# Batches 6 and 7 wholly by seven block products, denser two-batch products, and the last results stored by quarters

## The chip, the cores and the metric

The kernel runs on one core of a Trainium2 chip. The metric is the device time of one execution in microseconds, as the median of several runs. A core has a matrix engine (TensorE, PE in the profile; its weight loads are listed as PEld), VectorE (DVE), ScalarE (ACT), GpSimd (POOL) and SyncE (SP). Matrix products are written to PSUM, a small memory from which VectorE or ScalarE copies them to SBUF; DMA moves data between SBUF and device memory. A DMA is issued by an instruction in the queue of an engine, here SyncE, ScalarE or GpSimd (SPq, ACTq, POOLq).

## The reference

There are 8 batches of 1024 rows with 512 features, float32. A small network on the conditioning vector makes, per batch, a 512 x 512 matrix; a second layer scales its inputs and outputs per batch:

```python
# layer 0, per batch b
ae = layernorm(cond, ln_g, ln_b)
h  = gelu(ae @ w1 + b1)
x_a, x_b = split(h @ w2 + b2)              # each (8, 512, rank 8)
layer = base_layer + x_a @ x_b.T           # per batch
x = x + (x + x @ layer)                    # outer and inner residual
# layer 1, per batch b
ys = cond / sqrt(512)
d  = rsqrt((ys * ys) @ (weight * weight) + 1e-8)
x  = x + ((x * ys[b]) @ weight) * d[b]
```

Both layers are linear in x once the condition is known, so out[b] = x[b] @ Q[b], with one 512 x 512 matrix Q[b] per batch: (2 I + base + rank-8 term) times N[b], where N[b] = I + diag(ys) weight diag(d).

## The kernel before, in words

A float32 product is made of three fast ones. Each operand is split into a high part (rounded by a ScalarE cast) and the rest (a VectorE subtraction), and high x high, high x rest and rest x high are added up in PSUM. Every helper that prepares an operand therefore costs a cast and a subtraction.

**Setup (to about 81 us).** The conditioning network, the low-rank factors, and the matrices Q of batches 0 to 3 are made, the last three by `Base` with plain products.

**Main loop.** A step `i` is one tile of 128 rows: `main(b, t)` runs 4 chunks x 3 = 12 matmuls of 512 columns into a PSUM tile `po`, ScalarE copies it to `o`, and ScalarE issues the store. `load_x` fetches half a batch of x (1 MB, SyncE) and `split_x` splits two tiles. Other work is hung behind steps by `at(*place(i), f, ...)`: it is emitted after `main` of step i.

**Two-batch products (`Pair`).** Batches (4, 5) and (6, 7) share the left matrix, so their two matrices N form, side by side, a product of 2 x 2 blocks that needs seven block products instead of eight (`ORDER`, 14 units of 6 matmuls of 512 columns, tiles `pp`). The list `spots` gives the step behind which each unit is emitted. Ahead of a product, `early` makes its N blocks (VectorE), `prepare` forms their difference, rounds it and subtracts. The rounded operands have two buffers (`right_tiles`, tags `nh` and `nl`), so a product's operands can be made when the product two before it is over. After the last unit, `rank_term` adds the rank-8 term of each batch, and `split_p` splits Q into `ph` and `pl`.

**Seven block products (`Seven`).** Near the end the same scheme is used on the rows: half a batch (512 rows) is a product of 2 x 2 blocks, done by seven products of 12 matmuls of 256 columns (tiles `sw`, `sz`, `sv`). `make_sums` and `make_right` prepare the right side from Q; `make_left(g)` prepares half g, in six steps; `part(g, steps)` runs the seven products in the order 1, 5, 6, 2, 7, 3, 4 and takes one step of the next half's `make_left` after each. Products 1, 6, 7 and 4 accumulate in one bank (`w`; two banks, one per 128 rows, in the last part), 5 and 3 in bank `z`, 2 in bank `v`; after each product its running sum is copied out (ScalarE `copy` for 1, 5, 6, 4; VectorE `tensor_add` for 2, 7, 3). After product 3 the half `o1` is stored, after product 4 the half `o2`, by ScalarE. The raw sums share one buffer (tag `sums`).

Before, batches 0 to 5 and the first half of batch 6 go through the main loop (52 steps), and three halves through `Seven`: batch 6's second half, and both halves of batch 7.

**Order.** A build-time scheduler orders each engine's instructions by program order and readiness. Matmuls always keep program order. For VectorE, ScalarE and SyncE, `ve`, `se` and `sy` keep it only while `InOrder.on` is true: in setup, in `early`, and again in the closing parts. `late_pools` frees the pools of the making of Q and opens those of `Seven` in their place, along with a second output pool. Tiles named `big` (x, its split halves, Q, `xa`) share nine slots; `ph` and `pl` have two each.

Of the kernel before, what the change touches and what calls it, by code (L numbers as in the profile page):

```python
# [14 lines left out]
P = 128  # L15
NB = 8
NT = 1024
D = 512
# [12 lines left out]
def cond_resid_kernel(ctx: ExitStack, tc: tile.TileContext, small, cond, condrows, consts,  # L31
# [32 lines left out]
    ve, se, sy = InOrder(nc.vector), InOrder(nc.scalar), InOrder(nc.sync)  # L64
# [14 lines left out]
    def big_tile(name, dtype=F32):  # L79
        return big.tile([P, KC, D], dtype, tag="big", name=name)  # L80
# [82 lines left out]
    def newton_rsqrt(v, sd, shape, name):  # L163

        r = sp.tile(shape, F32, name=f"r_{name}")
        ve.reciprocal(r, sd)
        t = sp.tile(shape, F32, name=f"t_{name}")
        ve.tensor_mul(t, r, r)
        ve.tensor_mul(t, t, v)
        ve.tensor_scalar(t, t, -0.5, 1.5, ALU.mult, ALU.add)  # L170
        return r, t
# [12 lines left out]
    r, t = newton_rsqrt(ve_l, sd, [NB, 1], "l")  # L184
# [102 lines left out]
    r, t = newton_rsqrt(v, sv, [P, KC, NB], "d")  # L287
# [359 lines left out]
    def p_tiles(b):  # L647
        ph[b] = ppool.tile([P, KC, D], F32R, tag="ph", name=f"ph_{b}")
        pl[b] = ppool.tile([P, KC, D], F32R, tag="pl", name=f"pl_{b}")
# [13 lines left out]
    def load_x(b, h):  # L663
        raw[b, h] = big_tile(f"x_{b}_{h}")
        sy.dma_start(raw[b, h], x[b, h])

    def split_x(b, j, part=None):

        t = raw[b, j // 2][:, :, (j % 2) * 2 * P:(j % 2 + 1) * 2 * P]
        if part != 1:  # L670
            xs[b, j] = big.tile([P, 2, KC, 2 * P], F32R, tag="big", name=f"xs_{b}_{j}")
            se.copy(xs[b, j][:, 0], t)
        if part != 0:
            ve.tensor_sub(xs[b, j][:, 1], t, xs[b, j][:, 0].bitcast(F32))
# [136 lines left out]
    def main(b, t):  # L811
        s = xs[b, t // 2]
        at = slice((t % 2) * P, (t % 2 + 1) * P)
        ps = po.tile([P, D], F32, tag="po", name=f"po_{b}_{t}")
        for c in range(KC):
            for i, (u, m) in enumerate(((0, ph[b]), (0, pl[b]), (1, ph[b]))):
                mm(ps, s[:, u, c, at], m[:, c, :],
                   start=(c == 0 and i == 0), stop=(c == KC - 1 and i == 2))
        o = pools["o"].tile([P, D], F32, tag="o", name=f"o_{b}_{t}")
        se.copy(o, ps)  # L820
        nc.scalar.dma_start(out[b, t * P:(t + 1) * P, :], o)

    class Seven:
# [28 lines left out]
            self.right = {5: (h[:, 0], t[:, 0]), 6: (h[:, 1], t[:, 1]), 7: (h[:, 2], t[:, 2]),  # L852
                          4: (h[:, 3], t[:, 3])}

        def make_right(self, whole):

            b = self.b
            for rows, cols in ((slice(0, 4), slice(0, HD)), (slice(2, 4), slice(HD, D))):
                if whole:
                    break  # L860
                se.copy(ph[b][:, rows, cols], q[b][:, rows, cols])
                ve.tensor_sub(pl[b][:, rows, cols], q[b][:, rows, cols],
                              ph[b][:, rows, cols].bitcast(F32))
            for p, rows, cols in ((1, slice(0, 2), slice(0, HD)), (2, slice(2, 4), slice(0, HD)),
                                  (3, slice(2, 4), slice(HD, D))):
                self.right[p] = ph[b][:, rows, cols], pl[b][:, rows, cols]
# [49 lines left out]
        def part(self, g, steps=(), last=False):  # L916

            b, bank, steps = self.b, {}, iter(steps)
            o1, o2 = (pools["late"].tile([P, 2, D], F32, tag="o2", name=f"o{i}_{b}_{g}", bufs=3)
                      for i in range(2))  # L920
            for p in self.ORDER:
                key = {5: "z", 3: "z", 2: "v"}.get(p, "w")
                first = p in (1, 5, 2)
                if first:
                    pool, tag = (po, "po") if key == "z" else (acc, "acc")
                    bank[key] = [pool.tile([P, 2, HD], F32, tag=tag, name=f"s{key}{i}_{b}_{g}")
                                 for i in range(2 if key == "w" and last else 1)]
                self.product(g, p, bank[key], first)
                o, cols = {1: (o1, slice(0, HD)), 2: (o1, slice(0, HD)), 3: (o1, slice(HD, D)),
                           6: (o1, slice(HD, D)), 4: (o2, slice(0, HD)), 5: (o2, slice(HD, D)),  # L930
                           7: (o2, slice(HD, D))}[p]
                for m, u in enumerate(bank[key]):
                    u, to = (u, slice(0, 2)) if len(bank[key]) == 1 else (u[:, 0:1], slice(m, m + 1))
                    if p in (2, 3, 7):
                        ve.tensor_add(o[:, to, cols], u, o[:, to, cols])
                    else:
                        se.copy(o[:, to, cols], u)
                    if p in (3, 4):
                        self.store(o, g, int(p == 4), to)
                next(steps, None)  # L940

        def store(self, o, g, half, ms):
            at = g * HT + 2 * P * half
            se.dma_start(
                out[self.b, at + P * ms.start:at + P * ms.stop, :].rearrange("(m p) d -> p m d", p=P),
                o[:, ms, :])

    def late_pools():
        making.close()
# [3 lines left out]
    NTT = NT // P  # L953
    after = {}

    def at(b, t, f, *args):
        after.setdefault((b, t), []).append((f, args))
# [5 lines left out]
    place = lambda i: divmod(i, NTT)  # L963
# [4 lines left out]
        for j in range(2):  # L968
            at(*place(first + 3 + j), split_p, b, j)

    for b, spots in ((4, [11 + n for n in range(14)]), (6, [28 + 2 * n // 3 for n in range(14)])):
        first, end = spots[0], spots[-1] + 1
        at(*place(first - 9), load_d, b)
        at(*place(first - 6), new_pair, b)
        for n, p in enumerate(Pair.ORDER):
            spot = spots[2 * n]
            at(*place(spot - 5), lambda b=b, p=p: pairs[b].early(p))
            at(*place(spot - 2), lambda b=b, p=p: pairs[b].prepare(p))
        for spot in spots:
            at(*place(spot), lambda b=b: pairs[b].unit())  # L980
        at(*place(first + 2), load_rank, b)
        at(*place(first + 4), load_rank, b + 1)
        at(*place(end), rank_term, b)
        at(*place(end + 1), rank_term, b + 1)
    for b, spot in ((4, 26), (5, 33), (6, 41)):
        for j in range(2):
            at(*place(spot + j), split_p, b, j)
    sevens = [Seven(NB - 2), Seven(NB - 1)]
# [2 lines left out]
        for _ in sevens[i].make_left(g):  # L991
            pass

    at(*place(40), late_pools)
    at(*place(42), sevens[0].make_sums)
    at(*place(43), sevens[0].make_right, True)
    at(*place(44), load_x, NB - 2, 1)
    at(*place(45), sevens[1].make_sums)
    at(*place(47), all_left, 0, 1)
    at(*place(48), sevens[1].make_right, False)  # L1000
    at(*place(48), load_x, NB - 1, 0)

    HALF = NTT // 2
    TILES = (NB - 1) * NTT - HALF
    for i in range(TILES):
        b, t = divmod(i, NTT)
        if t == 0:
            p_tiles(b + 1)
        main(b, t)
        if t % 4 == 0 and i + 4 < TILES:  # L1010
            load_x(*divmod(i // 4 + 1, NHALF))
        if t % 2 == 0 and i + 4 < TILES:
            split_x(*divmod(i // 2 + 2, NTT // 2))
        for f, args in after.get((b, t), ()):
            f(*args)
    load_x(NB - 1, 1)
    InOrder.on = True
    sevens[0].part(1, sevens[1].make_left(0))
    sevens[1].part(0, sevens[1].make_left(1))
    sevens[1].part(1, last=True)  # L1020
# [69 lines left out]
```

## Time and profile before

| | |
|---|---|
| median of 3 runs | 302.38 us (302.2 to 302.98) |
| the profiled execution | 302.37 us |
| its span, first to last instruction | 300.6 us |
| mean granted TensorE clock | 0.997 |
| TensorE busy | 293.9 us, 98% of the span |
| VectorE, ScalarE, GpSimd busy | 206.0 (69%), 152.8 (51%), 34.8 (12%) |
| chain that ended last | PE 87%, DVE 5%, DMA 4%, ACT 2% |
| one step of the main loop (12 matmuls) | 2.72 us |
| one unit of a two-batch product (6 matmuls) | 1.36 to 1.40 us |
| one of the seven products of a half (12 matmuls) | 1.44 us |
| stores of 256 KB, issue to landing, median | 2.6 us |
| stores of 512 KB | 2.9 us |

In rows of the trace, the first number is the start, the second the length (microseconds from the start of the span), then engine, line, operation, output<-input, shape. A bracket at the end is idle time of the engine just before, with what ended it. Nearly all calls on VectorE, ScalarE and SyncE pass through line 62 and matmuls through line 45, so the tile names tell them apart. ACTq and SPq rows are DMA issues. Rows by stretch of time give, for each engine, its busy share and number of instructions (PE, PEld, DVE, ACT, POOL), then the granted clock, the DMA engines' busy share and GB/s. Ends of matmuls are modelled.

### The profile page before, as it was taken

How to read it: one execution, taken by the hardware profiler on the slowest of the kernel's cores; microseconds unless marked ns; L12 is line 12 of the kernel's file. 1: busy time of each engine (PE TensorE's matmuls, PEld its weight loads, DVE VectorE, ACT ScalarE, POOL GpSimd, SP SyncE). 2: the span in 40 equal slices, each digit the busy share in tenths (PEclk: the TensorE clock that was granted, in tenths of full speed). 3: DMA queues.
4: the chain of work that ended last, by engine and by line, in shares of the span. 5: the costliest groups of instructions: out<-in, count | busy, mean ns of one | idle time of the engine just before them, and what ended most of it. 6: DMA issues, size and time to landing. Idle time of an engine off the chain costs nothing.

```text
span 300.6 us, 3913 instructions
## 1 busy us (share of the span) xinstructions
PE 293.9 (98%) x1465; PEld 226.1 (75%) x1465; DVE 206.0 (69%) x303; ACT 152.8 (51%) x224; POOL 34.8 (12%) x74
## 2 busy tenths in 40 slices
PE   8999999999999999999999999999999999999993
PEld 3655465467878778888888778888887888899993
DVE  4779840979569999873564699855628379948721
ACT  4757132246556554575654444467532655653530
POOL 0011000057104550100000081000000000000000
PEclk9999999999999999999999999999999999999998
DMA  6999999696619986534525158243351729322133
GB/s 205 406 429 416 403 424 415 218 336 180 203 70 293 309 293 195 173 99 180 174 81 202 70 157 250 83 168 104 149 209 70 226 66 358 128 101 94 48 140 140
DMA packets 18995, 62.12 MB, mean 207 GB/s; under 512 B 2704, under 2 KB 2960, under 8 KB 14624
## 3 DMA queue, kind: packets, MB, share of 16 engines
q1 hardware_dynamic: 6064, 38.78, 35.2%
q10 hardware_dynamic: 9136, 16.78, 14.8%
q0 software_dynamic: 3776, 6.31, 8.0%
q8 instruction: 11, 0.18, 0.2%
q14 instruction: 8, 0.07, 0.1%
HBM read 44.02 MB, written 17.84 MB: 206 GB/s over the span
## 4 chain that ended last, share of the span: by engine, by line
PE 87%; DVE 5%; DMA 4%; ACT 2%; issue 0%; ACTq 0%
PE po L45 48%; PE pp L45 13%; PE pq L45 7%; PE sw L45 5%; DMA w<-in_w 4%; PE px L45 3%; PE sz L45 3%; PE warm L45 2%; PE pg L45 2%; DVE n L62 2%; PE sv L45 1%; PE pr L45 1%; PE pt_t L45 1%; ACT work L62 1%; DVE scr L62 0%
## 5 line engine op out<-in xcount | busy, mean ns | idle before, releaser
L45 PE MATMUL po<-ph,xs 128*128 128x512 f32 x416 | 134.3, 392 | 0.0
L45 PEld LDWEIGHTS po<-ph,xs 128*128 128x128 f32 x416 | 78.1, 188 | 18.0 <-issue 1.7
L45 PE MATMUL po<-pl,xs 128*128 128x512 f32 x208 | 81.1, 390 | 0.0
L62 ACT COPY o<-po 128x512 f32<-128x512 f32 x52 | 30.5, 586 | 58.0 <-PE po L45 58.0
L45 PEld LDWEIGHTS po<-pl,xs 128*128 128x128 f32 x208 | 39.1, 188 | 8.0
L62 DVE TENSOR_TENSOR xs<-x,xs 128x1024 fp32r<-128x1024 f32 x26 | 31.5, 1221 | 10.5 <-ACT xs L62 10.4
L62 ACT CAST xs<-x 128x1024 fp32r<-128x1024 f32 x26 | 27.0, 1051 | 2.6 <-DMA x<-in_x 1.3
L62 DVE TENSOR_TENSOR q<-pr,q 128x512 f32<-128x512 f32 x32 | 20.1, 684 | 7.4 <-PE pr L45 7.4
L62 DVE TENSOR_TENSOR nl_p<-n,nh_p 128x1024 fp32r<-128x1024 f32 x14 | 17.1, 1223 | 10.2 <-ACT nh_p L62 10.2
L62 DVE TENSOR_TENSOR pl<-q,ph 128x1024 fp32r<-128x1024 f32 (+1 forms) x16 | 18.8, 1189 | 6.9 <-ACT ph L62 6.8
L511 POOL DMA_DIRECT2D fa<-kept_a x28 | 13.7, 508 | 72.8 <-PE pr L45 72.7
L45 PE MATMUL pq<-nh,bh 128*128 128x512 f32 x48 | 19.8, 412 | 0.0
L45 PE MATMUL pq<-nl,bh 128*128 128x512 f32 x48 | 19.1, 398 | 0.1
L45 PE MATMUL pq<-nh,bl 128*128 128x512 f32 x48 | 19.0, 395 | 0.0
L62 DVE SCALAR_TENSOR_TENSOR n<-w_sb,ysT,d 128x512 f32<-128x512 f32 x24 | 17.8, 747 | 1.0 <-DMA d<-d_out 1.0
L62 ACT COPY q<-pp 128x512 f32<-128x512 f32 x20 | 11.8, 588 | 10.9 <-PE pp L45 10.9
L62 ACT CAST ph<-q 128x1024 fp32r<-128x1024 f32 (+1 forms) x16 | 16.2, 1027 | 2.1 <-DVE q L62 2.0
L45 PE MATMUL px<-w,hT 128*32 128x512 f32 x128 | 16.0, 601 | 0.1
L62 ACT CAST nh_p<-n 128x1024 fp32r<-128x1024 f32 x14 | 14.7, 1052 | 1.6 <-PE pp L45 1.6
L45 PEld LDWEIGHTS pq<-nh,bh 128*128 128x128 f32 x48 | 9.0, 188 | 8.4 <-issue 5.0
L511 POOL DMA_DIRECT2D ft<-kept_t x28 | 13.8, 519 | 5.0 <-DMA kept_t<-st_t 5.0
L62 ACT COPY o<-sw 128x512 f32<-128x512 f32 (+1 forms) x12 | 5.7, 480 | 15.7 <-PE sw L45 10.0
(185 smaller groups left out, 465.9 us busy)
## 6 DMA issues: line engine op xcount, KB each, us to landing
w<-in_w SPq DMA_DIRECT2D x16, 1024.0 KB, 10.8
x<-in_x SPq DMA_DIRECT2D x16, 1024.0 KB, 5.3
out<-o ACTq DMA_DIRECT2D x54, 256.0 KB, 2.6
out<-o ACTq DMA_DIRECT2D x5, 512.0 KB, 2.9
ft<-kept_t POOLq DMA_DIRECT2D x28, 64.0 KB, 3.0
fa<-kept_a POOLq DMA_DIRECT2D x28, 64.0 KB, 3.3
d<-d_out POOLq DMA_DIRECT2D x6, 256.0 KB, 4.6
w_sb<-in_weight SPq DMA_DIRECT2D x2, 512.0 KB, 5.4
```

The source lines that it names most:

```text
L45: tc.keep_in_program_order(nc.tensor.matmul(*args, **kw))
L62: return lambda *a, **kw: pin(f(*a, **kw)) if InOrder.on else f(*a, **kw)
L511: nc.gpsimd.dma_start(fold[name, b][32 * c:32 * c + 32, :], kept[name, g][32 * i:32 * i + 32, :])
```

## The change

Six things are edited.

- The main loop has 48 steps: batch 6's first half goes through `Seven` too, so four parts follow the loop. `p_tiles` of batches 6 and 7 is called by `make_right`, no longer by the loop, and `make_right` has lost its argument: before, it copied nothing for batch 6, whose `ph` and `pl` came from `split_p`; now it fills the three blocks that the products need for both batches.
- The units of the first pair are emitted behind steps 11 to 20 (before: 11 to 24), those of the second behind steps 24 to 32 (before: 28 to 36). `split_p` of batch 4 moves from steps 26, 27 to 27, 28; that of batch 6 goes.
- `late_pools` and `make_sums` of batch 6 come four steps earlier, its `make_right` two, `make_sums` of batch 7 three. `make_left` of batch 6's first half is emitted behind step 43, and x of batch 6 is loaded behind steps 42 and 46.
- After the loop `InOrder.on` is set; then come the load of batch 7's first half of x, part 0 of batch 6 (with `make_left` of its second half between its products), the load of batch 7's second half, `make_right` of batch 7, and the three parts that were there before. `make_right` of batch 7 stood behind step 48 before, with the order free.
- In the last part each finished quarter of results is stored on its own: that of product 2, the two row blocks of product 7 and the quarter of product 3 by SyncE, the two row blocks of product 4 by ScalarE. Before, ScalarE stored one whole half after product 3 and two row blocks after product 4.
- `store` takes the queue and the columns as arguments.

```diff
-        def make_right(self, whole):
+        def make_right(self):
             b = self.b
+            p_tiles(b)
             for rows, cols in ((slice(0, 4), slice(0, HD)), (slice(2, 4), slice(HD, D))):
-                if whole:
-                    break
                 se.copy(ph[b][:, rows, cols], q[b][:, rows, cols])
                 ve.tensor_sub(pl[b][:, rows, cols], q[b][:, rows, cols],
                               ph[b][:, rows, cols].bitcast(F32))
...
-                    if p in (3, 4):
-                        self.store(o, g, int(p == 4), to)
+                    if last and p in (2, 3, 7, 4):
+                        self.store(se if p == 4 else sy, o, g, int(p in (4, 7)), to, cols)
+                    elif p in (3, 4):
+                        self.store(se, o, g, int(p == 4), to, slice(0, D))
                 next(steps, None)
-        def store(self, o, g, half, ms):
+        def store(self, queue, o, g, half, ms, cols):
             at = g * HT + 2 * P * half
-            se.dma_start(
-                out[self.b, at + P * ms.start:at + P * ms.stop, :].rearrange("(m p) d -> p m d", p=P),
-                o[:, ms, :])
+            queue.dma_start(
+                out[self.b, at + P * ms.start:at + P * ms.stop, cols].rearrange("(m p) d -> p m d", p=P),
+                o[:, ms, cols])
...
-    for b, spots in ((4, [11 + n for n in range(14)]), (6, [28 + 2 * n // 3 for n in range(14)])):
+    for b, spots in ((4, [11 + 3 * n // 4 for n in range(14)]), (6, [24 + 2 * n // 3 for n in range(14)])):
...
-    for b, spot in ((4, 26), (5, 33), (6, 41)):
+    for b, spot in ((4, 27), (5, 33)):
         for j in range(2):
             at(*place(spot + j), split_p, b, j)
...
-    at(*place(40), late_pools)
-    at(*place(42), sevens[0].make_sums)
-    at(*place(43), sevens[0].make_right, True)
-    at(*place(44), load_x, NB - 2, 1)
-    at(*place(45), sevens[1].make_sums)
-    at(*place(47), all_left, 0, 1)
-    at(*place(48), sevens[1].make_right, False)
-    at(*place(48), load_x, NB - 1, 0)
-    HALF = NTT // 2
-    TILES = (NB - 1) * NTT - HALF
+    at(*place(36), late_pools)
+    at(*place(38), sevens[0].make_sums)
+    at(*place(41), sevens[0].make_right)
+    at(*place(42), load_x, NB - 2, 0)
+    at(*place(42), sevens[1].make_sums)
+    at(*place(43), all_left, 0, 0)
+    at(*place(46), load_x, NB - 2, 1)
+    TILES = (NB - 2) * NTT
     for i in range(TILES):
         b, t = divmod(i, NTT)
-        if t == 0:
+        if t == 0 and i + NTT < TILES:
             p_tiles(b + 1)
...
+    InOrder.on = True
+    load_x(NB - 1, 0)
+    sevens[0].part(0, sevens[0].make_left(1))
     load_x(NB - 1, 1)
-    InOrder.on = True
+    sevens[1].make_right()
     sevens[0].part(1, sevens[1].make_left(0))
     sevens[1].part(0, sevens[1].make_left(1))
     sevens[1].part(1, last=True)
```

## The prediction

> **What bounds the kernel now.** I read the page's first rows, then the chain of waits in order of time, then ScalarE, VectorE and DMA in the last 30 us. TensorE holds the chain; from 81 us on, pieces of it follow each other without a gap:
>
> ```profile
> PE 293.9 (98%) x1465; PEld 226.1 (75%) x1465; DVE 206.0 (69%) x303; ACT 152.8 (51%) x224; POOL 34.8 (12%) x74
> ```
> ```profile
> 254.93 10.88 PE po L45 x48
> 265.81 1.43 PE sw L45 x12
> 267.25 1.44 PE sz L45 x12
> 268.69 1.44 PE sw L45 x12
> 270.12 1.44 PE sv L45 x12
> 271.57 1.44 PE sw L45 x12
> 273.00 1.44 PE sz L45 x12
> 274.44 2.88 PE sw L45 x24
> ...
> 296.63 0.37 ACT o L62
> ```
>
> The columns are start and length. `po` are tiles of batch rows (48 matmuls = 4 tiles = 10.88 us, so 2.72 a tile); from 265.81 the seven block products of a half batch run, 1.44 us each. Only two kinds of edit can move the end: fewer TensorE microseconds or new waits on TensorE, and the tail after its last matmul, which ends at 296.04 (the last starts at 295.76 and is listed with 0.28); the span ends at 300.6, so the tail is 4.56 us.
>
> **1. Four tiles become seven products: -0.8 us.** 10.88 us go; 7 x 1.44 = 10.08 come ((296.04 - 265.81) / 21 products = 1.44). Here a rule speaks for more: the Trainium skill ("TensorE: Matmul & The Clock Gate", Back-to-back issue gap) gives 518 cycles at 2.4 GHz for 512 columns and 262 for 256, so 48 x 0.216 - 84 x 0.109 = 10.36 - 9.17 = -1.19. The rows have 0.227 and 0.120, some 11 ns over the page on each matmul, and the short form pays that 84 times instead of 48. I take the rows. The granted clock is 1.00 in all of these stretches, so neither side changes speed. On the helpers this step removes two `split_x` (1.05 ScalarE, 1.22 VectorE each), `split_p` of batch 6, four 0.59 us copies and four 256 KB stores, and adds `make_left(0)` (ScalarE 1.05 + 0.62 + 2 x 1.05 = 3.8; VectorE 4 x 0.69 + 3 x 1.22 + 0.69 = 7.1), four copies, three 0.69 us adds and two 512 KB stores. That is covered by the last tiles 43 to 47, 13.6 us; see the rival on the slower side for when it isn't.
>
> **2. `make_right` of batch 7 moves into the seam between the two halves of batch 6: +1.2 us.** Before, it stood after tile 48, unpinned, and ran at 259.45 on ScalarE and 260.73 on VectorE, under `po` tiles. Now it is pinned behind part 0 and ahead of part 1. It issues casts of 1024 and 512 elements and their two subtractions, no DMA. What it is put in front of is shown by the part that begins at 265.81 (ScalarE, then VectorE; start, length):
>
> ```profile
> 267.28 0.59 ACT L62 COPY o<-sw 128x512 f32<-128x512 f32 x1 [0.85 <-PE sw L45]
> 267.76 1.05 ACT L62 CAST xa<-x 128x1024 fp32r<-128x1024 f32 x1
> 268.71 0.62 ACT L62 CAST x<-x 128x512 fp32r<-128x512 f32 x1
> 269.23 0.59 ACT L62 COPY o<-sz 128x512 f32<-128x512 f32 x1
> 269.71 1.06 ACT L62 CAST sh<-sraw 128x1024 fp32r<-128x1024 f32 x1
> 270.66 0.60 ACT L62 COPY o<-sw 128x512 f32<-128x512 f32 x1
> ```
> ```profile
> 273.35 0.68 DVE L62 TENSOR_TENSOR o<-sw,o 128x512 f32<-128x512 f32 x1
> 273.95 0.68 DVE L62 TENSOR_TENSOR x<-x,x 128x512 fp32r<-128x512 f32 x1
> 274.55 0.68 DVE L62 TENSOR_TENSOR o<-sz,o 128x512 f32<-128x512 f32 x1
> 275.15 1.22 DVE L62 TENSOR_TENSOR sl<-sraw,sh 128x1024 fp32r<-128x1024 f32 x1
> ```
>
> Products 1, 6, 7 and 4 gather in one PSUM bank, and each may start only when the result before it has been copied out. So three margins exist: product 6 starts at 268.69, and copy 1 is done at 267.87 (0.82 spare); product 7 starts at 271.57, copy 6 is done at 271.26 (0.31); product 4 starts at 274.44, VectorE's add of product 7 is done at 274.03 (0.41). ScalarE is packed from copy 1 to copy 6, so what comes ahead of copy 1 reaches copy 6 whole. Count from the start of part 0, using this part as template: ScalarE ends part 0's last store at 11.11 (276.92 - 265.81). Its two casts then take 11.15 to 12.62 (issue steps 0.95 and 0.52, as above), so copy 1 of part 1 starts at 12.62 instead of 11.54: 1.08 late. Copy 6 is 1.08 late too and has 0.31 to spare: TensorE loses 0.77. That is the low end. VectorE adds to it: its subtractions wait for the first cast (12.2) and end at 14.0, the sums S1 and S2 that the cast `sh` needs end at 15.4, so `sh` runs at 15.43, copy 6 ends at 17.0 instead of the 15.8 at which product 7 was due: 1.2 lost. VectorE is then still late: its add of product 7 ends at 20.1, where product 4, already shifted, wants it at 19.9; 0.2 more. The high end is 1.45, some 1.6 if a stopped TensorE needs 0.05 at each of three restarts. I take 1.2: the ScalarE row alone is certain, VectorE's part hangs on S1 and S2 not having been issued ahead. Part 2 absorbs the rest: its first copy, at 23.0, finds ScalarE free at 22.8.
>
> **3. The tail: -1.3 us.** Now ScalarE holds the big last store (first row) ahead of both last copies, and the DMA engines carry 1 MB at once (second fence: busy share and GB/s close each row):
>
> ```profile
> 295.41 0.38 ACTq L62 DMA_DIRECT2D out<-o  x1
> 295.83 0.37 ACT L62 COPY o<-sw 128x256 f32<-128x256 f32 x1 [5.14 <-DVE o L62]
> 296.23 0.35 ACTq L62 DMA_DIRECT2D out<-o  x1
> 296.63 0.37 ACT L62 COPY o<-sw 128x256 f32<-128x256 f32 x1 [0.42 <-ACT o L62]
> 297.03 0.35 ACTq L62 DMA_DIRECT2D out<-o  x1
> ```
> ```profile
> 296.00:297.00 1.00, 0.04 (x1) 0.00 (x0) 0.00 (x0) 0.57 (x2) 0.00 (x0) 1.00 0.69 260
> 298.50:299.00 0.50, 0.00 (x0) 0.00 (x0) 0.00 (x0) 0.00 (x0) 0.00 (x0) 0.95 1.03 389
> 299.00:299.50 0.50, 0.00 (x0) 0.00 (x0) 0.00 (x0) 0.00 (x0) 0.00 (x0) 0.50 0.12 41
> ```
>
> The last store is issued at 297.03 and lands 2.5 later (299.53); 1.07 follow to the span's end. Afterwards half of `o1`, and `o2`'s product-7 half, have gone on SyncE's queue, which has nothing else then but x loads long issued. Product 3's quarter goes there too (issue 0.38, data near 296.3 to 297.0). On ScalarE: last matmul 296.04, copy 296.16 to 296.53, issue at 296.57, 0.46 earlier. Its 128 KB meet idle engines. Lone 256 KB stores under the `po` tiles land in 2.0; their data runs 0.67 of that, so half the bytes give an estimate of 1.7. Landing 298.25 against 299.53: -1.3. The upper bound of the gain is this; for the lower, rows of 1 KB might move no faster than the 86 KB `sm` load (1.9 to landing), and one queue could delay another by 0.2: -0.9. A rule speaks against this edit: the skill ("DMA: Bandwidth & Descriptors", Issuing engines are not separate DMA queues) has all queues on the same 16 engines, so that another issuer saves issue time only. By it alone the gain would be the 0.46; the rest comes from bytes being sent earlier, which the saturated windows here show is worth something.
>
> **4. Edits I cost at nothing.** The pairs: same 14 units of 1.36 us, same rank terms (0.68 of TensorE each with the slow restart). Operands of a product can be rounded only when the product two before it is done; at 14 units in 9 tiles that leaves 8.16 us for a 1.05 cast and a 1.22 subtraction, and the second pair already runs at that density from 182.5 to 226.4 with no gap. The first goes from 14 tiles to 10, 10.9 and 8.2 us of room, while VectorE was busy 24.2 of 33 us there; one late cast would cost its 1.05. The x loads move past nothing on SyncE that waits; 16 of them go out, the last two at 246.3, 19 us before use. `late_pools` and the `p_tiles` of batches 6 and 7 move with what uses them, and the tiles whose slots they take end (tiles 39 and 47) before they are written.
>
> **Sum.** -0.8 + 1.2 - 1.3 = -0.9 on a profiled 302.37 (span 300.6, 1.77 around it), equal to the median of 302.38 within 0.01. Forecast: **301.4**.
>
> **Rivals.** (B) The seam costs nothing, because the scheduler or idle slots let the casts pass: -0.8 - 1.3 = -2.1, 300.3. For it: ScalarE is idle 3.7 us before its last copy of each part. Against: `InOrder` pins both engines. 20%. (C) The seam costs its full 1.6 and the tail yields 0.9, the DMA latency being fixed: -0.1, 302.3. For it: VectorE has 9.1 us of work in a 10.08 us part already, 11.0 with `make_right`. 17%. (D) Slower: batch 6's first left blocks are not ready at the first product. Before, VectorE began the sums at 242.58, held 5.4 us by a store of the old output pool, and ended the left blocks at 260.82, 18.2 us later; now at most 4.3 us are added (`make_right`, two `split_x` that ran earlier), so a start later than 254.9 - 22.5 = 232.4 eats into part 0; product 5 is 1.4 into it and the forecast 0.9 + 0.9 from "slower", so a start at 235.6 decides. The old pool's last store is issued near 225.5 (tile 36 ends at 230.2 - 2 x 2.72 = 224.8) and, held as long as before, lands at 231: it would start in time. 8%, at 303.5. The likeliest (A) has 55%, its own range 300.9 to 301.9.
>
> **Chances and range.** 0.3% is about what a measurement of this kernel tells from no change: 301.47 to 303.29 is "same". A lies over the edge by 0.32 of its 0.55, B is faster, C same, D slower: faster 0.52, same 0.40, slower 0.08. Leaving out D and the ends of B and C: 300.1 to 302.5.
>
> **What would show it.** Seven `sw/sz/sv` pieces more and 48 `po` matmuls fewer (step 1); after the eighth product a `ph` cast ahead of a copy, and TensorE gaps of 0.3 to 0.9 before products 6, 7, 4 of part 1 (step 2; without them B is right); last store issued about 0.55 after the last matmul, DMA idle between quarters, tail near 3.3 (step 3); gaps in `pp` pieces between 115 and 162 would refute step 4.

## The result: no measurable change

The changed kernel takes 302.29 us (median of 14 runs, 301.87 to 304.04), the kernel before, measured beside it, 302.37 us (301.86 to 302.98). The ratio is 1.0003, 95% interval 0.9990 to 1.0017. The forecast was 301.4 us, with 300.1 to 302.5 as the range, 52% on "faster" and 40% on "same": the time lies inside the range, but the gain of 0.9 us did not come. Three of the 14 runs of the changed kernel lie at 303.2 to 304.0; why is not shown.

The profiled execution of the changed kernel took 302.08 us with a span of 300.3. First the chain of waits in order of time, from the end of the loop (start, length):

```profile
254.59 1.43 PE sw L45 x12
...
263.23 1.45 PE sw L45 x12
...
264.70 0.59 ACT o L62
...
265.74 1.06 ACT ph L62
...
270.01 1.05 ACT sh L62
271.06 0.49 ACT o L62
...
271.60 1.32 PE sw L45 x9
...
279.56 1.23 DVE xa L62
280.79 0.00 issue
280.79 1.05 ACT sh L62
281.84 0.49 ACT o L62
...
282.38 1.69 PE sw L45 x12
```

In the kernel before, this stretch was TensorE without a break. Here part 0 (254.59 to 264.68) runs at 1.44 us a product; then the chain leaves TensorE for ScalarE's `ph` casts and returns at 271.60, and a second time at 282.38.

The loop lost what it was to lose: in the chain's pieces, from the first `po` to the first product, it takes 254.59 - 80.52 = 174.07 us, before 265.81 - 80.89 = 184.92, so 10.85 less for four tiles. From there to the last matmul's end (297.03) are 42.44 us, where four parts of 10.08 would be 40.32. The tail is 300.3 - 297.03 = 3.27 us, before 4.56. Counted from the loop's start, TensorE ends 1.36 us later (216.51 against 215.15) and the tail is 1.29 shorter. The two cancel; the 0.3 us by which the two spans differ is the loop's earlier start in this execution (80.52 against 80.89), which scatters from 80.5 to 81.4 over the nine kernels profiled here.

The TensorE rows of part 1, one matmul each; a bracket is the idle time before it:

```profile
267.26 0.28 PE L45 MATMUL sz<-th,sl 128*128 128x256 f32 x1
267.84 0.39 PE L45 MATMUL sw<-th,sh 128*128 128x256 f32 x1 [0.30 <-ACT o L62]
268.07 0.28 PE L45 MATMUL sw<-tl,sh 128*128 128x256 f32 x1
...
270.70 0.28 PE L45 MATMUL sv<-ph,xa 128*128 128x256 f32 x1
271.60 0.39 PE L45 MATMUL sw<-th,sh 128*128 128x256 f32 x1 [0.61 <-ACT o L62]
...
274.46 0.28 PE L45 MATMUL sz<-ph,sl 128*128 128x256 f32 x1
274.71 0.38 PE L45 MATMUL sw<-th,x 128*128 128x256 f32 x1
274.93 0.28 PE L45 MATMUL sw<-tl,x 128*128 128x256 f32 x1
```

Matmuls in step start 0.12 apart. Product 6 starts 0.58 after its predecessor (0.46 lost), product 7 0.90 (0.78 lost), product 4 0.25 (0.13 lost), and after each stop the second matmul comes 0.22 or 0.23 later instead of 0.12: another 0.10 per restart. The sum is 1.68 us. The ScalarE rows of the same time show who was in front:

```profile
265.32 0.38 ACTq L62 DMA_DIRECT2D out<-o  x1
265.74 1.57 ACT L62 CAST ph<-q 128x1024 fp32r<-128x1024 f32 x2 [0.45 <-ACT o L62]
267.21 0.58 ACT L62 COPY o<-sw 128x512 f32<-128x512 f32 x1
...
270.01 1.05 ACT L62 CAST sh<-sraw 128x1024 fp32r<-128x1024 f32 x1 [0.27 <-DVE sraw L62]
270.97 0.58 ACT L62 COPY o<-sw 128x512 f32<-128x512 f32 x1
...
275.88 0.38 ACTq L62 DMA_DIRECT2D out<-o  x1
...
280.31 0.59 ACT L62 COPY o<-sz 128x512 f32<-128x512 f32 x1 [0.38 <-DMA out<-o]
```

The two casts of batch 7's right side sit between the last store of part 0 and copy 1 of part 1. VectorE is late for the same reason (`sraw` rows are the sums of the left blocks, here S2; the last row is the add of product 7, for which product 4 waits):

```profile
266.82 1.82 DVE L62 TENSOR_TENSOR pl<-q,ph 128x1024 fp32r<-128x1024 f32 x2 [1.68 <-ACT ph L62]
...
269.29 0.69 DVE L62 TENSOR_TENSOR sraw<-sraw,x 128x512 f32<-128x512 f32 x1
...
273.97 0.68 DVE L62 TENSOR_TENSOR o<-sw,o 128x512 f32<-128x512 f32 x1
```

The cast `sh` starts at 270.01, when S2 is done.

The last ScalarE row above is the second, unforeseen stop: in part 2 the copy of product 5 waits 0.38 us for an output buffer, whose store was issued at 275.88 and landed 4.3 us later, and product 7 starts late again. From copy 4 of part 1 (276.44) to that of part 2 (286.99) are 10.55 us instead of 10.08: 0.47 lost. The chain of waits names VectorE at this place, because its subtraction for `xa` ends just when the cast `sh` starts (280.79). The cast does not need it: in part 1 it ran at 270.01, on S2 alone and ahead of that subtraction, and in part 2 S2 was done at 278.4. What held it is the late copy in front of it.

The tail, as ScalarE sees it:

```profile
297.20 0.37 ACT L62 COPY o<-sw 128x256 f32<-128x256 f32 x1 [0.48 <-PE sw L45]
297.60 0.35 ACTq L62 DMA_DIRECT2D out<-o  x1
```

The last copy follows TensorE directly, its store is issued 0.57 after the last matmul (before: 0.99) and lands 1.7 later (before: 2.5).

### The profile page after: what moved, and what is told of

Its sections match the earlier page's. It is cut to its first block, busy times and chain, and to the rows that moved or that the text cites. A ratio compares the mean times of both kernels' runs of the same rounds, so it can differ in the third digit from the quotient of the medians.

```text
span 300.3 us, 4005 instructions
## 1 busy us (share of the span) xinstructions
PE 293.4 (98%) x1501; PEld 227.1 (76%) x1501; DVE 211.0 (70%) x312; ACT 154.1 (51%) x226; POOL 34.8 (12%) x74
## 4 chain that ended last, share of the span: by engine, by line
PE 84%; DVE 9%; ACT 3%; DMA 2%; issue 1%; SPq 0%; ACTq 0%
PE po L45 44%; PE pp L45 13%; PE pq L45 10%; PE sw L45 5%; PE px L45 4%; PE sz L45 2%; PE pg L45 2%; DVE n L62 2%; DMA b_raw<-in_baseT 2%; DVE sraw L62 1%; PE pr L45 1%; PE sv L45 1%; ACT o L62 1%; DVE sl L62 1%; ACT sh L62 1%
## 5 line engine op out<-in xcount | busy, mean ns | idle before, releaser
L45 PE MATMUL po<-ph,xs 128*128 128x512 f32 x384 | 123.8, 392 | 0.0
L45 PEld LDWEIGHTS po<-ph,xs 128*128 128x128 f32 x384 | 72.1, 188 | 16.8 <-issue 1.7
L45 PE MATMUL po<-pl,xs 128*128 128x512 f32 x192 | 74.8, 389 | 0.0
L62 ACT COPY o<-po 128x512 f32<-128x512 f32 x48 | 28.1, 586 | 52.8 <-PE po L45 52.8
L45 PEld LDWEIGHTS po<-pl,xs 128*128 128x128 f32 x192 | 36.1, 188 | 7.4
L62 DVE TENSOR_TENSOR xs<-x,xs 128x1024 fp32r<-128x1024 f32 x24 | 29.0, 1221 | 10.5 <-ACT xs L62 10.4
L62 ACT CAST xs<-x 128x1024 fp32r<-128x1024 f32 x24 | 24.9, 1052 | 3.7 <-DMA x<-in_x 1.9
L511 POOL DMA_DIRECT2D fa<-kept_a x28 | 13.7, 502 | 64.9 <-PE pr L45 64.8
L62 ACT COPY o<-sw 128x512 f32<-128x512 f32 (+1 forms) x15 | 7.5, 500 | 19.2 <-PE sw L45 14.4
```

What stands on the lines that cost most here:

```text
L45: tc.keep_in_program_order(nc.tensor.matmul(*args, **kw))
L62: return lambda *a, **kw: pin(f(*a, **kw)) if InOrder.on else f(*a, **kw)
L511: nc.gpsimd.dma_start(fold[name, b][32 * c:32 * c + 32, :], kept[name, g][32 * i:32 * i + 32, :])
```

## The experiments

Theory: the place of `make_right` in the order of ScalarE and VectorE takes back what seven products and the tail bring. Rivals: VectorE is simply full; the loss lies in the denser pairs; the tail's gain is not what it seems. All times are medians; the kernel before, measured beside each, stands at 302.34 us for the first two experiments and the two on the tail, and at 302.26 for the other three.

**Casts in ScalarE's idle stretch.** ScalarE is idle for 3 us of each part ahead of its store. `make_right` is divided into casts and subtractions:

```diff
+    def between(steps, extra):
+        for n, _ in enumerate(steps):
+            for f in extra.get(n, ()):
+                f()
+            yield
...
-    sevens[0].part(0, sevens[0].make_left(1))
+    sevens[0].part(0, between(sevens[0].make_left(1), {3: [casts], 5: [rests]}))
     load_x(NB - 1, 1)
-    sevens[1].make_right()
     sevens[0].part(1, sevens[1].make_left(0))
```

> The changed kernel with make_right of batch 7 taken apart: its two casts go into ScalarE's idle stretch of part 0, after product 2, its two subtractions behind the last step of make_left, still ahead of part 1. Theory (the seam costs TensorE 1.67 us in part 1 and, by a later store, 0.47 in part 2): no TensorE gap in parts 1 and 2, last matmul 2.1 us earlier after the last loop tile, 302.3 - 2.1 = 300.2 us. Rival 1 (VectorE's 11 us of work in a 10 us part is the limit, whoever casts when): gaps stay at products 7 and 4, 301.5 or more. Rival 2 (the loss lies before the loop's end, in the denser pairs): no gain beyond 0.5 us.

Measured: 300.54 us, ratio 0.9944 (0.9932 to 0.9956). The chain of waits has no stop in part 1 any more, and one in part 2:

```profile
264.03 2.88 PE sw L45 x24
266.91 1.44 PE sz L45 x12
268.35 1.44 PE sw L45 x12
269.79 1.44 PE sv L45 x12
271.23 1.47 PE sw L45 x12
...
274.93 4.61 DMA out<-o
```

The first row holds product 4 of part 0 and product 1 of part 1 back to back. Against the changed kernel's median 1.75 us are gained. In the traces, part 1 takes 10.09 us from copy 4 to copy 4 instead of 11.74, so the seam's loss is gone, and VectorE, with the same work as before, is not in the way: rival 1 and rival 2 fall. The expected 300.2 is missed by 0.3, because the wait for the output buffer stays (part 2 takes 10.70): the store lands in 4.6 us although it is now issued on time. I had taken that wait for a consequence of the seam, and it is not one. (The execution profiled is the slowest of the six, 301.5 us; its loop starts 0.8 later, at 81.35.)

**Only VectorE's half moved.** The casts stay at the seam, the subtractions come two steps later:

```diff
-    sevens[1].make_right()
-    sevens[0].part(1, sevens[1].make_left(0))
+    casts()
+    sevens[0].part(1, between(sevens[1].make_left(0), {1: [rests]}))
```

> The changed kernel with only VectorE's half of make_right moved: the casts stay at the seam, the two subtractions come after S3 and S4 of batch 7's left blocks. It tells ScalarE's share from VectorE's. Theory (ScalarE's queue alone makes copy 1 and copy 6 late by 1.1): product 6 still waits 0.45, product 7 some 0.4 instead of 0.78, product 4 not at all; with 0.1 per restart about 1.05 us lost in part 1 instead of 1.67, so 301.7 us, or 301.2 if the output buffer is free in time. Rival (VectorE's lateness is the cause): about 300.5 us.

Measured: 301.47 us, ratio 0.9976 (0.9967 to 0.9986). From copy 4 of part 0 (264.96) to copy 4 of part 1 (276.11) are 11.15 us, 1.07 more than 10.08, as expected from ScalarE's queue alone (1.05). In the chain of waits `sh` now runs right behind copy 5, and product 4 follows product 3 without a gap:

```profile
269.52 0.48 ACT o L62
270.00 0.95 ACT sh L62
...
274.63 2.88 PE sw L45 x24
```

So of the 1.68 us, some 1.07 are ScalarE's and 0.6 come on top through VectorE. The output buffer comes almost in time here (part 2 takes 10.12 us), the case for which 301.2 was expected; the time lies between the two figures.

**The same work one part earlier.**

```diff
     load_x(NB - 1, 0)
+    sevens[1].make_right()
     sevens[0].part(0, sevens[0].make_left(1))
     load_x(NB - 1, 1)
-    sevens[1].make_right()
```

> The changed kernel with make_right of batch 7 whole, pinned ahead of part 0 instead of ahead of part 1. Theory (it is the place in ScalarE's queue ahead of copy 1 that costs): the casts run from 1.0 to 2.5 us after the last loop tile, copy 1 of part 0 is 1.0 late, products 6 and 7 of part 0 wait 0.4 and 0.7 and 0.1 for each restart, product 4 not, as VectorE has S1 to S4 done: 1.3 lost instead of 1.67, 301.9 us. Rival (only the seam between the parts is full): nothing lost, 300.6 us.

Measured: 302.27 us, ratio 0.9998 (0.9990 to 1.0007): the whole loss has moved with it. The size was expected as 1.3 and is 1.6 (copy 4 of part 0 is at 266.79; part 0 starts at 255.06, and 10.08 later is 265.14). The reason is in the VectorE rows: S1 to S4 were not issued ahead, they stand pinned behind the subtractions, which wait 6.75 us for the cast.

```profile
257.17 1.83 DVE L62 TENSOR_TENSOR pl<-q,ph 128x1024 fp32r<-128x1024 f32 x2 [6.75 <-ACT ph L62]
258.91 0.68 DVE L62 TENSOR_TENSOR sraw<-x 128x512 f32<-128x512 f32 x1
```

**The tail alone.** The kernel before with `store` and its calls as in the change, and nothing else.

> The kernel before with only the last part's stores changed (quarters, partly by SyncE). Theory: last store issued 0.5 us after the last matmul instead of 1.0, DMA idle when it comes, 4.56 us of tail become 3.27: 302.4 - 1.3 = 301.1 us. Rival (the 1 MB is over in time anyway, only ScalarE's issue time is saved): 301.9 us.

Measured: 301.43 us, ratio 0.9969 (0.9957 to 0.9981), 0.9 us gained, between the two expectations. The stores do what was expected: the last is issued at 296.55, 0.58 after the last matmul ends at 295.97, and lands in 1.7. But 1.35 us then pass until the span's end, where the kernel before has 1.07 and the changed one 1.0. What fills this rest is not shown.

**The change without the tail's stores.** In the changed kernel, ScalarE stores halves and row blocks as before.

> The changed kernel with the stores of the last part as before (one half by ScalarE, then two row blocks). Theory: the tail's gain is the same with the rest of the change in place, so 302.3 + 1.3 = 303.6 us. Rival (the tail's gain is only of use because TensorE ends later): 302.8 us or less.

Measured: 303.95 us, ratio 1.0050 (1.0037 to 1.0063): 1.7 us more than the changed kernel, against an expected 1.3. Without the tail's stores the change would be slower than the kernel it started from. The two runs on the tail agree on the stores themselves: from the last matmul's end to the last landing are 3.5 us with the old stores, in the kernel before and in this one (297.15 to 300.6), and 2.3 with the new ones, on either base, so 1.2 are gained. The rest, from there to the span's end, made 0.9 of it in one case (1.07 grew to 1.35) and 1.7 in the other, where it fell from 1.6 to 1.0.

**What the denser pairs are worth.** The kernel with the casts in the idle stretch, with pairs and preparation at their old steps:

```diff
-    ... (4, [11 + 3 * n // 4 ...]), (6, [24 + 2 * n // 3 ...])
+    ... (4, [11 + n ...]), (6, [28 + 2 * n // 3 ...])
-    at(*place(36), late_pools)
-    at(*place(38), sevens[0].make_sums)
-    at(*place(41), sevens[0].make_right)
-    at(*place(42), sevens[1].make_sums)
+    at(*place(40), late_pools)
+    at(*place(42), sevens[0].make_sums)
+    at(*place(43), sevens[0].make_right)
+    at(*place(45), sevens[1].make_sums)
```

(`split_p` of batch 4 is back at step 26 too.)

> The kernel with the casts in ScalarE's idle stretch, but both two-batch products at their old places (behind steps 11 to 24 and 28 to 36), and late_pools, make_sums and make_right of batch 6 where they stood before (40, 42, 43), make_sums of batch 7 at 45. It asks what the denser pairs are worth. Theory: they change nothing in the loop itself, but give the preparation of batch 6's first half its time: without them the sums start near 242.6, VectorE needs 14 us of work that took 18 before, and TensorE, at the end of its loop at 254.9, waits 2 to 5 us for product 5's and 7's operands: 302.5 to 305 us. Rival (the preparation has room anyway): 300.5 us, the same as with denser pairs.

Measured: 303.7 us (302.02 to 305.14), ratio 1.0037 (1.0022 to 1.0052), 3.2 us more than with denser pairs. It scatters much more than its neighbours. Its profiled execution, at 302.02, is the best of 20. There VectorE begins the sums at 241.00, after a wait for a store of the old pool, and the left blocks are ready at 252.1 (second row, `sl`), still 2.7 us before part 0 starts at 254.8. What is late is ScalarE: it rounds the sums of batch 7 (`th`) ahead of the last copies of the loop, and copy 1 of part 0 comes at 257.99:

```profile
241.00 1.29 DVE L62 TENSOR_TENSOR traw<-q 128x512 f32<-128x512 f32 x2 [4.54 <-DMA out<-o]
...
249.72 2.36 DVE L62 TENSOR_TENSOR sl<-sraw,sh 128x1024 fp32r<-128x1024 f32 x2 [0.39 <-ACT sh L62]
```
```profile
254.05 2.00 ACT L62 CAST th<-traw 128x1024 fp32r<-128x1024 f32 x2 [1.88 <-DMA out<-o]
...
257.99 0.58 ACT L62 COPY o<-sw 128x512 f32<-128x512 f32 x1 [0.41 <-PE sz L45]
```

Products 6 and 7 of part 0 stop for it, and copy 4 comes 1.7 us late (266.62 instead of 264.9). So the time was the expected one, but the operands of products 5 and 7 were not what TensorE waited for; what the slower executions wait for is not shown. In the changed kernel the sums start at 231.10, and the left blocks are ready at 249.7, 4.9 us before part 0. The denser pairs cost nothing in the loop (174.07 us from its first `po` to part 0 in both kernels); together with the earlier preparation, which this run moved back with them, they keep ScalarE free at the start of part 0.

**Quarters in every part.** On top of the first experiment, all parts store as the last one does:

```diff
-                    if last and p in (2, 3, 7, 4):
+                    if p in (2, 3, 7, 4):
                         self.store(se if p == 4 else sy, o, g, int(p in (4, 7)), to, cols)
-                    elif p in (3, 4):
-                        self.store(se, o, g, int(p == 4), to, slice(0, D))
```

> The kernel with the casts in ScalarE's idle stretch, and now every part stores by quarters, as the last one does. Theory: what is left in that kernel is one wait of product 5's copy in part 2 for an output buffer, whose 512 KB store lands in 4.6 us instead of 2.9, because one of the 16 DMA engines is busy for 1 to 1.7 us with a 16 KB instruction packet when this store and the next are under way; with a last quarter of 256 KB the buffer is free in time, so TensorE has no gap in part 2 and 300.54 - 0.5 = 300.0 us. Rival: the engine that is behind delays the quarter as well, no gain, 300.5 us.

Measured: 300.32 us, ratio 0.9936 (0.9923 to 0.9948). In the profiled execution TensorE has no stop left in any part; ScalarE's copy of product 5 in part 2 follows the cast before it:

```profile
277.88 0.62 ACT L62 CAST x<-x 128x512 fp32r<-128x512 f32 x1
278.39 0.59 ACT L62 COPY o<-sz 128x512 f32<-128x512 f32 x1
```

In the trace part 2 takes 10.09 us instead of 10.70. The medians differ by 0.2 us instead of the expected 0.5, with ranges that overlap (300.1 to 300.97 and 300.31 to 301.5), so the size of the gain is not settled. This version is 2 us faster than both kernels of the study.

## Why the prediction came out as it did

**Step 1, seven products for four tiles (-0.8).** Right: 10.85 us went and the added part takes 10.09. The price per matmul in the Trainium skill ("TensorE: Matmul & The Clock Gate", Back-to-back issue gap), which the page gives for an isolated gap, would have made it -1.19; the trace's rows held.

**Step 2, the seam (+1.2).** The mechanism was right to the instruction: casts ahead of copy 1, the three waits at products 6, 7 and 4, and ScalarE and VectorE caught up by part 2. The size was the term that failed: 1.68 us measured, 0.08 over the high end. I took a middle value between 0.77 and 1.45 to 1.6, on the ground that S1 and S2 might have been issued ahead; they were not (S2 at 269.29, behind the subtractions), and in a pinned order they couldn't be. The worked-out schedule of ScalarE held: it put copy 6's end at 17.0 after the part's start, and it was 271.55 - 254.59 = 16.96.

Two smaller readings were off. The spare times 0.82, 0.31 and 0.41 were taken to the pieces of the chain, but a product's first matmul starts some 0.16 us ahead of its piece. In the kernel before, products 6, 7 and 4 start thus:

```profile
268.52 0.28 PE L45 MATMUL sw<-th,sh 128*128 128x256 f32 x1
...
271.40 0.29 PE L45 MATMUL sw<-th,sh 128*128 128x256 f32 x1
...
274.28 0.28 PE L45 MATMUL sw<-th,x 128*128 128x256 f32 x1
```

So only 0.65, 0.14 and 0.25 were to spare, and up to product 7's start 1.34 were lost (0.46 + 0.10 + 0.78) instead of 1.2. And each restart took 0.10 instead of 0.05. Product 4's own stop was smaller than worked out, 0.13 instead of 0.2.

**What the sum lacked: 0.47 us in part 2.** I had followed the shift to ScalarE's first copy, but not to the next thing that was late, the release of the output buffer. Even so it would have fitted with the 2.9 us that such stores took before: 275.88 + 2.9 = 278.8, a microsecond ahead of 279.9, when ScalarE was ready for product 5's copy. The landing time is the part that changed.

**Step 3, the tail (-1.3).** Right in the changed kernel: the tail is 3.27 us, 1.29 less than 4.56, and the last store takes 1.7 to landing as estimated from half the bytes. The stores alone are worth 1.2 on both bases; with the stretch after the last landing, which differs between kernels for a reason not shown, the same edit brought 0.9 on the kernel before and 1.7 on the changed one.

**Step 4, edits at nothing.** Right for the loop: 174.07 us agree with 184.92 less four tiles to 0.03. The rival for "slower", left blocks not ready, did not occur: the sums start at 231.10, where 231 was worked out. With pairs and preparation at their old steps the left blocks are ready too, in the execution profiled; there it is ScalarE's casts for batch 7 that cost time.

**The sum.** -10.85 + 10.08 + 1.68 + 0.47 - 1.29 = +0.09 us; the medians differ by -0.08, and the interval of the ratio allows -0.3 to +0.5. The likeliest case was too low by 0.9. Rival C gave this time (302.3) with the full seam, but with a tail of 0.9 and no buffer wait: its seam was right, and that its total fits is luck, because the 0.4 it took too little for the tail and the 0.47 it lacked cancel.

## What to carry to other kernels

When an edit shortens the bound engine, look at which copies that engine waits for and how much spare time each has, counted to the first matmul that needs it: here 0.65, 0.14 and 0.25 us, and 1.5 us of casts put in front of them cost more than the edit brought. Work that has to be pinned somewhere belongs where its engine waits anyway; the same casts and their subtractions cost 1.7 us at the seam, and nothing once the casts stood three products earlier. When a bound has been worked out step by step, take its worked-out value rather than the middle of the range, and follow the delay past the first engine that recovers, to buffers and their stores.

## What the runs showed of the hardware

A pair of 512 KB stores that landed in 2.9 us each in the kernel before landed in 3.7 to 4.6 in part 1 of all six kernels with four parts that store halves there. The pairs of parts 0 and 2 in the same six kernels landed in 2.8 to 3.0. The DMA summary of the changed kernel for 276.6 to 281.0, then of the kernel before for the pair at the same place (276.0 to 279.5):

```profile
q10 hardware_dynamic: 543, 1.05, 64.3%
q8 instruction: 1, 0.02, 1.4%
```
```profile
q10 hardware_dynamic: 544, 1.05, 79.7%
```

One packet of the queue named "instruction" (16 KB, 0.96 us long) falls into the pair, at 277.2. The stretches after it (DMA share and GB/s at the end of the row):

```profile
279.00:279.50 0.50, 0.50 (x7) 0.50 (x6) 0.50 (x2) 0.50 (x2) 0.00 (x0) 1.00 1.01 381
279.50:280.00 0.50, 0.50 (x7) 0.50 (x6) 0.50 (x2) 0.43 (x1) 0.00 (x0) 1.00 0.15 53
280.00:280.50 0.50, 0.50 (x7) 0.50 (x6) 0.50 (x1) 0.19 (x1) 0.00 (x0) 1.00 0.06 25
280.50:281.00 0.50, 0.50 (x6) 0.50 (x6) 0.28 (x1) 0.50 (x2) 0.00 (x0) 1.00 0.07 29
```

Fifteen engines are done at 279.6; for another 1.4 us a share of 0.06 to 0.07, one sixteenth, is still busy, and the second store, issued at 277.06, lands only after that, at 281.5. The Trainium skill ("Advanced Engine Details and Errata", ISA Cache) has instruction lines of 16 KB for 256 instructions; the packets in the parts come 16.0 and 15.7 us apart in the changed kernel, 13.7 and 16.9 in the first experiment, about the 15.4 us of 128 weight loads and 128 matmuls at 0.12, so they may belong to TensorE's stream, which 36 more matmuls have shifted against the stores. That is an estimate. That the packet delays its engine was argued from the coincidence: six kernels have the packet at the slow pair and at no other pair, two have it at none. In the kernel with quarters everywhere it falls at the same place, and the 256 KB store there lands in 3.2 us instead of the 2.2 in part 2. Moving the packet alone was not tried.
